# Neighbour averages with three blocks of targets to a product instead of four

## The chip, the cores and the metric

The kernel runs on one core of a Trainium2 chip. The metric is the device time of one execution in microseconds. Before the change it was 3845.87 us, the median of three runs (3844.31 to 3850.38).

## What is computed

The reference is a small graph network on 6250 nodes with 128 features. There are 206,250 directed edges: 100,000 drawn pairs, both ways, and a loop on every node, sorted by target. A first part with two message layers is followed by a second part, in which each of three layers takes the mean of a node's neighbours. The second part is the one that matters here:

```python
def _L1_gnn_ref(x, edge_index, Wl, bl, Wr):
    src = edge_index[0]
    dst = edge_index[1]
    n = x.shape[0]
    deg = jax.ops.segment_sum(jnp.ones(src.shape[0], dtype=x.dtype), dst, num_segments=n)
    inv_deg = (1.0 / jnp.maximum(deg, 1.0))[:, None]
    h = x
    for i in range(NUM_LAYERS):
        agg = jax.ops.segment_sum(h[src], dst, num_segments=n) * inv_deg
        h = agg @ Wl[i].T + bl[i] + h @ Wr[i].T
        if i < NUM_LAYERS - 1:
            h = jax.nn.relu(h)
    return h
...
x = x + _L0_gnn_ref(relu(layernorm(x)), edge_index, ...)
x = x + _L1_gnn_ref(relu(layernorm(x)), edge_index, ...)
```

## The kernel before

Nodes are cut into blocks of B = 128, which gives NB = 49 blocks. All of the work is in the function `fast`; a slow general way, `general`, is compiled too and not run on these data.

The first part sorts the edges of each target block and runs the two message layers (to 2913 us). In its second layer it also counts, for each pair of a source block and a target block, how many edges join each source to each target. These counts, 128 x 128 bytes for each pair of blocks, go to the array `cnt` in HBM, in the order target block, source, source block, target.

The second part, the averages (lines 731 to 787), turns every segment sum into dense products with these counts. For a group of n target blocks, `sums = sum over the 49 source blocks s of h[s]^T x cnt[s -> group]`, where the columns of a product are the n x 128 targets of the group. This document calls the work on one group a **pass**. The features `h` are kept as two parts (`h2`, the index k), which add up to the exact value, so that each source block takes two products: a pass has 2 x 49 = 98 products, all into one PSUM bank `p` of 512 columns, which is the reason for at most four blocks. `spans` lists the groups as (first block, number of blocks): eleven groups of four, then one of three and one of two, since a last group of one is avoided. The three layers run over the same list.

In the order of the code, a pass does the following:

- Every R = 8 source blocks it loads the counts of its n target blocks into a byte tile `c8` (L767). The load stands on SP's queue. There are three buffers (the pool `mats` has `bufs=3`), so seven loads per pass, the last one for a single source block.
- Every K = 4 source blocks it turns the bytes into 32-bit numbers, `cf` (L771). ScalarE and VectorE take turns at this cast through the whole stage (`turn`); a pass has 13 casts, so that the engine that begins alternates from pass to pass. `cf` too has three buffers, and the last cast of a pass, of a single source block, takes a whole one.
- After every third source block it calls `next(behind, None)`, which lets the work on the previous pass's nodes go one step on.
- It issues the two products of the source block (L779).

At the end of a pass what is left of the previous pass's `behind` is finished, and a new one begins for this pass: `averaged` copies the PSUM bank to `sums` on ScalarE (L737), then takes the n blocks one after the other. For each, TensorE multiplies by `Wl` (L742, two instructions), VectorE scales by the inverse degree and adds the rest, giving `u` (L744); in the first two layers `mean_rows` follows, with a rounding of `u` to `h2` on ScalarE (L264) and its remainder on VectorE (L265), a transpose on TensorE (L268), a copy of it on ScalarE (L270), and the product with `Wr` (L273, two instructions) whose result VectorE adds to the bias (L274). In the third layer there is instead a load of `x1d` (L750), an addition (L751) and the store of the output (L753), both DMAs on SP's queue. The document calls this the **side work** of a node block. In the trace it is interleaved with the products, six products from one step to the next, and the first L742 of a pass comes after four or ten of its products.

Each engine takes its instructions in order. What is behind a waiting instruction on the same queue waits too.

Of the kernel before, what the change touches and what calls it, by code (L numbers as in the profile page):

```python
# [45 lines left out]
@with_exitstack  # L46
def gnn_kernel(ctx: ExitStack, tc: tile.TileContext, x, src, dst, weights, columns, rows, out, edges):

    nc = tc.nc
    dram = ctx.enter_context(tc.tile_pool(name="dram", bufs=1, space=DRAM))
    const = ctx.enter_context(tc.tile_pool(name="const", bufs=1))
    ident = const.tile([D, D], F32, name="ident")
    make_identity(nc, ident)
    miss_i = const.tile([1, 1], I32, name="miss_i")
    fast(tc, dram, ident, miss_i, x, src, dst, weights, columns, rows, out, edges)  # L60
    tc.strict_bb_all_engine_barrier()
    missed = nc.values_load(miss_i[0:1, 0:1], min_val=0, max_val=1,
                            skip_runtime_bounds_check_because="a comparison's result")
    with tc.If(missed > 0):
        general(tc, dram, ident, x, src, dst, weights, columns, rows, out)


def fast(tc, dram, ident, miss_i, x, src, dst, weights, columns, rows, out, edges):
    nc = tc.nc
    N = x.shape[0]  # L70
    NB = N // B
# [9 lines left out]
    with ExitStack() as ctx:  # L81
# [672 lines left out]
                yield  # L754

        turn = 0
        spans = [(g, min(4, NB - g)) for g in range(0, NB, 4)]
        if spans[-1][1] == 1:
            spans[-2:] = [(NB - 5, 3), (NB - 2, 2)]
        for l in range(3):  # L760
            for g, n in spans:
                p = bank("pe")
# [253 lines left out]
```

## Time and profile before

| | |
|---|---|
| median of the runs | 3845.87 us |
| the profiled execution: its time | 3845.1 us |
| the profiled execution: its span, first to last instruction | 3843.3 us |
| busy: TensorE, VectorE, ScalarE | 98%, 76%, 66% of the span |
| mean granted clock of TensorE | 0.996 |
| the averages: from their first product to the last | 2912.99 us to 3831.2 us |
| DMA in the averages | 118 to 158 GB/s in the slices wholly of that stage |

The stage splits by layer and by pass as follows. Each figure is the time from the first product of a pass to the first of the next, by the starts in the trace (of the very last, to the end of its last product).

| | first pass | passes of four after it | pass of three | pass of two | whole layer |
|---|---|---|---|---|---|
| first layer | 24.75 us | 10, 25.14 to 25.22 us | 20.12 us | 16.25 us | 312.9 us |
| second layer | 25.69 us | 9, 25.13 to 25.22 us, and one of 25.46 | 19.66 us | 14.43 us | 311.8 us |
| third layer | 24.45 us | 10, 23.82 to 23.83 us | 18.14 us | 12.60 us | 293.5 us |

A pass of four in the first two layers holds 98 products and the side work of four node blocks (8 instructions of L742, 4 of L268, 8 of L273). The pass of three and the pass of two carry the nodes of the pass before them, so four and three. The second and the third layer begin with the two nodes of the last pass of the layer before. The idle time at the end of the first layer is 2.13 us, and at the end of the second 0.57 us; both lie in the figures of the passes of two.

How to read it: TensorE is the engine to follow. A row of the groups gives the line, engine and operation, the tiles and shapes, the number of instructions, then the busy time, the mean duration of one and the idle time of the engine ahead of them with what ended it. The chain of waits follows the work that ended last back through whatever released it. In the timeline, columns are the start in us, the duration in us, the engine, the line and the operation; what ended an idle time is in brackets.

### The profile page before, as it was taken

The page shows a single profiled execution, that of the slowest core. Times are in us where ns is not written, and L with a number is a line of the kernel's source. Part 1 is how long each engine was busy: PE and PEld are TensorE (multiplying, and loading weights), DVE is VectorE, ACT ScalarE, POOL GpSimd, SP SyncE. Part 2 cuts the span into 40 slices and gives each one's busy share as a digit, 9 for nine tenths or more (in the row PEclk, how much of TensorE's full clock was granted, in tenths as well). Part 3 has the DMA queues.
Part 4 walks back from the last instruction along what each step waited for, and adds up shares of the span by engine and source line. Part 5 has one row for each costly group of instructions (what it writes and reads, how often), then busy time and mean ns, then how long its engine had stood idle before and what let it go on. Part 6 is the DMA issues. An engine that isn't in the chain of part 4 may idle for free.

```text
span 3843.3 us, 117274 instructions
## 1 busy us (share of the span) xinstructions
PE 3785.3 (98%) x45975; PEld 3570.6 (93%) x45975; DVE 2901.7 (76%) x7367; ACT 2522.5 (66%) x4869; POOL 1.0 (0%) x8
## 2 busy tenths in 40 slices
PE   6999999999999999999999999999999999999998
PEld 4999999999999999999999999999998888888887
DVE  8999999999999997787777778787874444444443
ACT  7565666566655665777877788787875555555554
POOL 0000000000000000000000000000000000000000
PEclk9999999999999999999999999999999999999999
DMA  4555555555555555677777777777774444444554
GB/s 139 161 166 169 170 175 164 168 172 175 165 168 170 173 170 169 204 212 213 215 212 215 211 217 210 212 216 213 214 212 136 131 129 118 129 128 121 157 158 131
DMA packets 656081, 671.11 MB, mean 175 GB/s; under 512 B 113201, under 2 KB 504475, under 8 KB 655387
## 3 DMA queue, kind: packets, MB, share of 16 engines
q1 hardware_dynamic: 650124, 662.26, 57.8%
q8 instruction: 362, 5.93, 0.6%
q10 hardware_dynamic: 5390, 1.26, 0.2%
q14 instruction: 205, 1.67, 0.1%
HBM read 534.28 MB, written 128.99 MB: 173 GB/s over the span
## 4 chain that ended last, share of the span: by engine, by line
PE 96%; DVE 2%; DMA 1%; ACT 1%; issue 0%; SPq 0%; DVEq 0%; ACTq 0%
PE pe L779 22%; PE pe L563 21%; PE pe L565 21%; PE agg L583 21%; PE so L522 4%; PE so L418 2%; PE mm L273 1%; PE agg L742 1%; PE mm L600 1%; PE mm L601 1%; PE mm L252 1%; PE mm L268 0%; DMA a<-in_x 0%; PE mm L616 0%; PE mm L595 0%
## 5 line engine op out<-in xcount | busy, mean ns | idle before, releaser
L563 PE MATMUL pe<-a,ot 128*128 128x128 bf16 x14700 | 1626.2, 219 | 0.0
L565 PE MATMUL pe<-b,ot 128*128 128x128 bf16 x14700 | 1620.5, 219 | 0.0
L563 PEld LDWEIGHTS <-ot 128*128 128x128 bf16 x14700 | 1036.5, 98 | 33.2
L565 PEld LDWEIGHTS <-ot 128*128 128x128 bf16 x14700 | 1026.6, 98 | 0.0
L779 PE MATMUL pe<-cf,h 128*128 128x512 f32 (+2 forms) x3822 | 911.3, 391 | 2.7 <-ACT cf L771 2.0
L779 PEld LDWEIGHTS pe<-cf,h 128*128 128x128 f32 x3822 | 675.3, 189 | 131.8 <-ACT cf L771 2.6
L572 ACT ACTIVATE m<-pe 128x512 fp32r<-128x512 f32 (+1 forms) x882 | 507.6, 576 | 321.0 <-PE pe L565 277.1
L489 DVE TENSOR_SCALAR ot<-v_all,part 128x1024 bf16<-128x1024 bf16 (+1 forms) x1274 | 599.4, 471 | 145.2 <-PE pe L565 127.6
L771 ACT CAST cf<-c 128x2048 fp32r<-128x2048 uint8 (+4 forms) x253 | 433.7, 1714 | 330.4 <-PE pe L779 273.8
L583 PE MATMUL agg<-m,hd_r 128*128 128x256 f32 (+1 forms) x3332 | 613.0, 303 | 0.5 <-DVE m L552 0.5
L552 DVE SCALAR_TENSOR_TENSOR m<-pe,m 128x512 fp32r<-128x512 f32 (+1 forms) x882 | 577.3, 655 | 18.8 <-ACT m L572 5.1
L771 DVE CAST cf<-c 128x2048 fp32r<-128x2048 uint8 (+4 forms) x254 | 285.7, 1125 | 351.8 <-PE pe L779 212.7
L583 PEld LDWEIGHTS agg<-m,hd_r 128*128 128x128 f32 x3332 | 452.0, 190 | 1.0 <-DVE m L552 0.9
L583 PE MATMUL agg<-m,hd 128*128 128x129 f32 x3136 | 434.5, 281 | 0.0
L514 ACT CAST hd_r<-hd_b 128x512 fp32r<-128x512 bf16 (+1 forms) x637 | 393.2, 618 | 2.0 <-DMA hd_b<-ohd 2.0
L583 PEld LDWEIGHTS agg<-m,hd 128*128 128x128 f32 x3136 | 380.9, 191 | 0.0
L524 ACT CAST ca<-so 128x512 uint8<-128x512 f32 (+1 forms) x637 | 358.9, 563 | 0.0
L514 ACT CAST hd<-hot 128x512 f32<-128x512 bf16 x392 | 242.7, 619 | 169.6 <-DVE hot L88 66.5
L575 ACT ACTIVATE m<-pe 128x512 f32<-128x512 f32 x392 | 234.0, 597 | 143.5 <-PE pe L565 141.7
L88 DVE TENSOR_TENSOR hot<-sv,iota 128x512 bf16<-128x512 f16 (+1 forms) x637 | 249.3, 404 | 29.3 <-ACT hd_r L514 22.2
L88 DVE TENSOR_TENSOR hs<-sources,iota 128x512 bf16<-128x512 f16 (+1 forms) x637 | 259.1, 407 | 2.8 <-PE so L522 1.5
L522 PE MATMUL so<-hd_b,hs 128*128 128x128 bf16 x2450 | 244.3, 219 | 2.1 <-DMA hd_b<-ohd 1.5
(162 smaller groups left out, 3136.6 us busy)
## 6 DMA issues: line engine op xcount, KB each, us to landing
v_all<-svd SPq DMA_DIRECT2D x1176, 256.0 KB, 3.9
c<-cnt SPq DMA_DIRECT2D x198, 512.0 KB, 3.7
ohd<-hot SPq DMA_DIRECT2D x588, 128.0 KB, 3.6
hd_b<-ohd SPq DMA_DIRECT2D x588, 128.0 KB, 3.7
cnt<-ca SPq DMA_DIRECT2D x540, 64.0 KB, 3.7
v_all<-svd SPq DMA_DIRECT2D x98, 128.0 KB, 3.2
c<-cnt SPq DMA_DIRECT2D x18, 384.0 KB, 3.2
c<-cnt SPq DMA_DIRECT2D x18, 256.0 KB, 2.8
```

Of the source, the lines that this page charges most:

```text
L88: nc.vector.tensor_tensor(to, v.rearrange("p (r e) -> p r e", e=2).unsqueeze(2).to_broadcast([B, n, B, 2]), iota_2.unsqueeze(1).to_broadca ...
L489: nc.vector.tensor_scalar(t[:, :n].rearrange("p j k s -> p (j k) s"), v[:, :2 * n], part, None, op0=OP.is_equal)
L514: nc.scalar.copy(hd[:, :n].rearrange("p (r e) v -> p r e v", e=2), hot[:, :n // 2].rearrange("p r v e -> p r e v"))
L522: nc.tensor.matmul(pa[:, j * B:(j + 1) * B], source[:, j // 2, :, j % 2], target[:, j // 2, :, j % 2], start=True, stop=True)
L524: nc.scalar.copy(ca[:, :n], pa[:, :n * B].rearrange("p (j d) -> p j d", d=B))
L552: nc.vector.scalar_tensor_tensor(m[:, :n, :D], pe, 0.0, m[:, :n, D:2 * D].bitcast(F32), op0=OP.max, op1=OP.subtract)
L563: nc.tensor.matmul(pe[:, o], t[:, j, 0, :], a3[l][:, block, k, :], start=(k == 0), stop=False)
L565: nc.tensor.matmul(pe[:, o], t[:, j, 1, :], b3[:, k, :], start=False, stop=(k == 2))
L572: nc.scalar.activation(m[:, :n, D:2 * D], pe, AF.Relu)
L583: nc.tensor.matmul(to, hd[:, j, :], m[:, j, :to.shape[1]], start=(c == 0), stop=(c == NB))
L771: (nc.scalar.copy if turn % 2 else nc.vector.tensor_copy)(cf[:, :k, :n].rearrange("p s w d -> p w s d"), c8[:, :n, s % R:s % R + k])
L779: nc.tensor.matmul(p[:, :n * B], h2[l % 2][:, s, k, :], cf[:, s % K, :n].rearrange("p w d -> p (w d)"), start=(s == 0 and k == 0), stop=(s ...
```

## The change

The list of groups is built with three blocks to a group instead of four. For 49 blocks that gives groups that begin at 0, 3, ... 48, of which the last would hold one block; the last two are replaced by (45, 2) and (47, 2). So there are 15 passes of three and two of two in each layer, 17 instead of 13. Nothing else in the code is changed: tiles and buffers keep their sizes, a product has 384 columns instead of 512, a load brings 384 KB instead of 512 KB, and a cast turns 1536 numbers per partition instead of 2048.

```diff
         turn = 0
-        spans = [(g, min(4, NB - g)) for g in range(0, NB, 4)]
+        spans = [(g, min(3, NB - g)) for g in range(0, NB, 3)]
         if spans[-1][1] == 1:
-            spans[-2:] = [(NB - 5, 3), (NB - 2, 2)]
+            spans[-2:] = [(NB - 4, 2), (NB - 2, 2)]
         for l in range(3):
             for g, n in spans:
                 p = bank("pe")
```

Per layer this makes 1666 products instead of 1274, 221 casts instead of 169, 119 loads of counts instead of 91, and 17 copies of sums instead of 13. The number of node blocks, and with it the side work, is 49 in either case.

## The prediction

> **What bounds the kernel now.** I read the page's chain of waits first, then the groups with shapes apart from 2900 us to the end, then the timeline of a few stretches.
>
> ```profile
> PE 96%; DVE 2%; DMA 1%; ACT 1%; issue 0%; SPq 0%; DVEq 0%; ACTq 0%
> ```
>
> TensorE sets the end. The chain gives L779, the products that the change reshapes, 22% of the span; they run from 2912.99 us on, and nothing before that is touched.
>
> ```profile
> L779 PE MATMUL pe<-cf,h 128*128 128x512 f32 x3234 | 815.2, 404 | 2.7 <-ACT cf L771 2.0 <-DVE cf L771 0.4 <-PE mm L616 0.3
> L771 ACT CAST cf<-c 128x2048 fp32r<-128x2048 uint8 x198 | 376.9, 1904 | 258.7 <-PE pe L779 229.8 <-issue 24.2 <-DVE u L744 2.3
> L771 DVE CAST cf<-c 128x2048 fp32r<-128x2048 uint8 x198 | 242.8, 1226 | 275.6 <-PE pe L779 158.7 <-ACT cf L771 86.5 <-issue 23.7
> L779 PE MATMUL pe<-cf,h 128*128 128x384 f32 x294 | 57.3, 344 | 0.0
> L779 PE MATMUL pe<-cf,h 128*128 128x256 f32 x294 | 39.7, 287 | 0.0
> L771 ACT CAST cf<-c 128x1536 fp32r<-128x1536 uint8 x18 | 26.5, 1475 | 20.1 <-PE pe L779 16.7 <-issue 3.4
> L771 DVE CAST cf<-c 128x1536 fp32r<-128x1536 uint8 x18 | 22.0, 1224 | 19.3 <-PE pe L779 16.5 <-issue 2.6
> L771 ACT CAST cf<-c 128x1024 fp32r<-128x1024 uint8 x18 | 18.9, 1048 | 16.5 <-PE pe L779 14.2 <-issue 2.3
> L737 ACT COPY sums<-pe 128x512 f32<-128x512 f32 x33 | 19.2, 583 | 7.9 <-PE pe L779 7.9
> L737 ACT COPY sums<-pe 128x384 f32<-128x384 f32 x3 | 1.4, 473 | 0.6 <-PE pe L779 0.6
> ```
>
> Two readings. Products hardly wait for casts (2.7 us in 3234) while casts wait for products, so casts have room. And each layer already has one pass of three blocks and one of two: the trace holds the new shapes, three passes of each. A matmul's mean (404 ns) overlaps its neighbours, so I price products by their spacing, from unbroken stretches of the chain:
>
> ```profile
> 3639.80 18.74 PE pe L779 x80
> ...
> 3805.91 12.65 PE pe L779 x73
> ...
> 3821.90 8.10 PE pe L779 x69
> ```
>
> That is 234.25 ns with 512 columns, 173.3 with 384, 117.4 with 256: per block of 128, 58.6, 57.8 and 58.7 ns.
>
> **The products.** A layer has now 11 passes of four, one of three, one of two, 98 products each: 98 x (11 x 234.25 + 173.3 + 117.4) = 281.0 us. Afterwards 15 of three and two of two: 98 x (15 x 173.3 + 2 x 117.4) = 277.8. That is 3.25 less per layer, 9.7 less in three, although 392 products per layer are added.
>
> [...]
>
> **Side work.** Behind each pass TensorE does the previous pass's nodes (L742, L268, L273). In the third layer two pairs of L742 start at 3661.63 and 3663.25 with six products between: 1.62 - 6 x 0.234 = 0.22 us per node. In the first two, steady passes of four last 25.13 to 25.22 us between their first products; less 98 x 0.234 = 22.96 that is 0.56 per node. Nodes stay 49 a layer, so this moves and costs nothing more. Even these passes hold no waiting.
>
> **Waits.** What a pass takes beyond products and side work, from the starts of first products:
> - passes of three: 20.12 - 16.98 - 4 x 0.555 = 0.91; 19.66 gives 0.45; third layer 18.14 - 16.98 - 0.88 = 0.27.
> - passes of two, without the idle end: 0.93, 0.67, and in the third layer about 0.42 with the last product's tail.
> - first passes: 1.44 (products 427 ns apart at the start), 1.62 and 0.38; one pass of four 0.28; idle ends of layers 2.13 and 0.57.
> Together 10.2 us now; the same ledger closes on the stage's length within 0.1.
>
> Where the 0.91 lies shows the mechanism:
>
> ```profile
> 3201.73 1.23 DVE L771 CAST cf<-c 128x1536 fp32r<-128x1536 uint8 x1 [0.41 <-PE pe L779]
> 3201.88 0.38 PE L742 MATMUL agg<-wt,sums 128*128 128x128 f32 x2
> ...
> 3202.87 0.34 DVE L744 SCALAR_TENSOR_TENSOR u<-agg,inv,hT 128x128 f32<-128x128 f32 x1
> ...
> 3203.26 0.33 PE L268 MATMUL mm<-ident,u 128*128 128x128 f32 x1
> ```
>
> L268 needs u, u is queued on VectorE behind a cast, and the six products between now last 1.04 us instead of 1.41; the next spacing was 295 instead of 173 ns, and at the third node 470. VectorE's cast of 1536 costs what 2048 costs (1224, 1226 ns): its share per pass rises while cover shrinks. Behind L268 all products queue in order. At a pass's start the first L742 waits for the sums copy (316 and 213 ns instead of 173 and 109), which shrinks with the copy, 0.58 to 0.47.
>
> A new pass of three carries three nodes, not four. The first three nodes of the two samples waited 0.61 and 0.41; less 0.1 for the shorter copy, between 0.3 and 0.5. Bounds: 0.1 (the start alone) and 0.9 (the worst sample at every pass). I take 0.45, nearer the samples' mean than either end. Third layer 0.2 (0.05 to 0.27). After: first passes 1.44 + 0.95 + 0.4; 28 x 0.45 = 12.6; 14 x 0.2 = 2.8; passes of two 0.8 + 0.55 in each of the first two layers, 0.67 in the third, 0.1 for the new handover from two to two.
>
> **Ends of layers.**
>
> ```profile
> 3223.93 1.90 ACT L771 CAST cf<-c 128x2048 fp32r<-128x2048 uint8 x1 [1.94 <-PE pe L779]
> ...
> 3225.88 1.48 PE L779 MATMUL pe<-cf,h 128*128 128x512 f32 x4 [1.96 <-ACT cf L771]
> ```
>
> ```profile
> c<-cnt SPq DMA_DIRECT2D x198, 512.0 KB, 3.7
> c<-cnt SPq DMA_DIRECT2D x18, 384.0 KB, 3.2
> c<-cnt SPq DMA_DIRECT2D x18, 256.0 KB, 2.8
> ```
>
> The named releaser is long done: the load was issued at 3220.09, when its buffer came free, and the cast began 3.83 later. With 384 KB the load is 0.5 and ScalarE's cast 0.43 shorter: idle 2.13 becomes about 1.2, and 0.57 (VectorE's cast first) about 0.06. After the 2.13 the layer's first products ran 427 ns apart; after 0.57 they did not. Whether 1.2 does is not in the trace: bounds 0 and 1.6 us, and I take half, which is the 0.95 above.
>
> [...]
>
> **Costed at nothing.** Loads rise from 91 to 119 per layer, 28 x 0.36 us on SP's queue, which is idle most of the stage; bytes stay. The tightest load is a pass's second: its buffer comes free with the cast of blocks 44 to 47 of the pass before, and from the release of that cast to its own cast 26 products pass, 4.5 us, less the 1.5 of the cast: 3.0, against 3.2 to land. The 0.2 is covered, since that cast is due 16 products (2.77) after the pass begins and needs 0.35 + 1.48 of them; in the third layer, where loads stand behind L750 and L753 on SP, a further 0.7 would be, and the rest paid in full. Four more copies on ScalarE per layer (0.47 each) lie under products; uncovered, 12 x 0.47 = 5.6.
>
> **Sum.** Waits after: 1.44 + 0.95 + 0.4 + 12.6 + 2.8 + 2.7 + 0.67 + 0.1 + 1.2 + 0.06 = 22.9, 12.7 more than 10.2. With -9.7 the stage is 3.0 longer: the profiled run of 3845.1 (span 3843.3) becomes 3848.1; that run lies 0.8 below the median 3845.87, which becomes **3848.8**.
>
> **Rivals.**
> - A, cheaper products without new waits. For: passes of four show none, so the order on the queues can be free of them. Against: all three passes of three show some. With 0.1 and 0.05 per pass: 3848.8 - 28 x 0.35 - 14 x 0.15 = 3836.9.
> - B, slower: u behind VectorE's cast at every pass. For: 0.91 in one sample, and a cast that does not shrink. With 0.9 per pass, 0.27 in the third layer: 3848.8 + 28 x 0.45 + 1 = 3862.4. It decides from about 0.6 per pass on.
> - C, slower: casts late at the start of a pass. The last block's lone cast takes a whole buffer, so the next pass's casts have 10 products' time, 1.73 us, against 1.475 on ScalarE; with 1.17 against 1.05, passes of two lost some 0.14 to 0.19, so the handover costs about 0.3 and three blocks just fit. Were it 0.5: 45 x 0.25 = 11 us, 3860.
> - D, the price of 173.3 does not hold and 384 columns cost what a line through 256 and 512 gives, 175.8: 4410 x 2.5 ns = 11, 3860. Against: 73 products in a row at 173.3.
> The change does what it says: 15 x 3 + 2 + 2 = 49 blocks.
>
> **How the numbers follow.** Forecast 0.55, A 0.12, B 0.22, C 0.05, D 0.06. The forecast's own range is 3842 to 3855 (0.25 to 0.65 per pass). The whole range leaves out most of A and the top of B: 3838 to 3862. No change means within 0.2%, 7.7 us, about what a measurement can tell: 3838.2 to 3853.6. Faster is A, 0.12; slower is B, C, D and 0.03 of the forecast, 0.36; the rest 0.52.
>
> **What would show it.** 4410 products with 384 columns at 173 ns in unbroken stretches (D if near 176); passes of three some 19.1 us long in the first two layers and 17.8 in the third (A at 18.7, B at 19.5); spacings before L268 and L273 longer than 173 (B), or before the fifth or ninth product of a pass (C); idle ends of 1.2 and 0.1 us. I would be wrong if casts or loads, not side work, filled the passes' extra time, or if work before 2913 us moved.

## The result, and the profile after

| | before | after |
|---|---|---|
| median of 20 runs of each on one chip | 3845.96 us (3841.03 to 3851.61) | 3852.48 us (3849.78 to 3857.04) |
| ratio after to before | | 1.0019 [1.0012, 1.0025] |
| profiled execution: time, span | 3845.1, 3843.3 us | 3851.8, 3850.0 us |
| start of the first product of the averages | 2912.99 us | 2912.72 us |
| **stage**: from there to the end of the last product | 918.2 us | 926.0 us |
| **tail**: from there to the end of the span | 12.1 us | 11.3 us |

The change makes the kernel 6.5 us slower: clear of zero, and by the medians just inside the 0.2% that the prediction called no change (the interval reaches 0.25%). The stage is 7.8 us longer, the tail 0.8 shorter, the start 0.27 earlier; that is the 6.7 us between the spans. TensorE still sets the end; VectorE's share of the chain of waits went from 2% to 3%:

```profile
PE 95%; DVE 3%; DMA 1%; ACT 1%; issue 0%; SPq 0%; DVEq 0%; ACTq 0%
```

The groups of the averages of the kernel after, shapes apart (instructions, then busy time and mean ns of one, then idle time before them):

```profile
L779 PE MATMUL pe<-cf,h 128*128 128x384 f32 x4410 | 835.1, 344 | 2.2 <-DVE cf L771 1.3 <-ACT cf L771 0.8
...
L771 ACT CAST cf<-c 128x1536 fp32r<-128x1536 uint8 x270 | 398.5, 1476 | 305.0 <-PE pe L779 227.3 <-issue 72.6 <-DMA c<-cnt 3.8
L771 DVE CAST cf<-c 128x1536 fp32r<-128x1536 uint8 x270 | 330.5, 1224 | 260.2 <-PE pe L779 227.4 <-DMA c<-cnt 19.1 <-issue 7.6
L779 PE MATMUL pe<-cf,h 128*128 128x256 f32 x588 | 78.0, 286 | 0.7 <-DVE cf L771 0.7
```

A product with 384 columns takes the 344 ns that it took before, and 79 of them in a row in the chain of waits last 13.71 us, so 173.5 ns each: the price that was forecast.

```profile
3637.87 13.71 PE pe L779 x79
```

ScalarE's cast shrank with the block, from 1904 to 1476 ns. VectorE's did not, 1226 to 1224, and VectorE now makes 270 of these where it made 198: it is busy longer for the same counts. The loads now end 19.1 us of the idle time ahead of VectorE's casts.

By passes, as in the table of before:

| | first pass | passes of three after it | passes of two | whole layer |
|---|---|---|---|---|
| first layer | 19.79 us | 13, 19.08 to 19.15 (by turns 19.15 and 19.12), one of 19.85 | 13.78, 14.53 us | 316.6 us |
| second layer | 18.38 us | 13, 19.13 to 19.28, one of 19.53 | 14.27, 13.54 us | 314.8 us |
| third layer | 18.60 us | 13, 17.79 to 17.85, one of 18.40 | 13.53, 12.32 us | 294.5 us |

Products by their spacing are 3 x 277.8 = 833.3 us. With side work at the prediction's 0.555 and 0.22 us per node, some 65 us, the waits of the stage are 27.5 us: 10.2 before, 22.9 forecast.

**Where a pass waits.** Three places, each read in the timeline of the kernel after (start, duration, engine, line, operation; in brackets the idle time before it and what ended it). First, the start of a pass:

```profile
3007.51 1.48 ACT L771 CAST cf<-c 128x1536 fp32r<-128x1536 uint8 x1 [1.30 <-PE pe L779]
...
3009.05 0.65 PEld L779 LDWEIGHTS pe<-cf,h 128*128 128x128 f32 x4 [0.20 <-ACT cf L771]
3009.21 0.48 ACT L737 COPY sums<-pe 128x384 f32<-128x384 f32 x1 [0.21 <-PE pe L779]
```

ScalarE's cast could begin only when a buffer of cf came free, and its end is what the next weight load and product waited for: one spacing of 280 ns instead of 173, 0.107 us in every pass of three. Second, in every other pass:

```profile
3017.22 0.38 PE L742 MATMUL agg<-wt,sums 128*128 128x128 f32 x2
...
3017.42 1.22 DVE L771 CAST cf<-c 128x1536 fp32r<-128x1536 uint8 x1 [0.76 <-PE pe L779]
3018.56 0.34 DVE L744 SCALAR_TENSOR_TENSOR u<-agg,inv,hT 128x128 f32<-128x128 f32 x1
...
3018.96 0.33 PE L268 MATMUL mm<-ident,u 128*128 128x128 f32 x1
```

L742 gives agg, but u (L744) is queued on VectorE behind a cast that began first, and L268, on which every later product waits, starts only with u: 470 ns instead of 173 in front of it, 0.35 us in all. Third, in the passes between, uT (L270) is queued on ScalarE behind a cast of 1.48 us in the same way, and L273 waits:

```profile
3033.55 1.48 ACT L771 CAST cf<-c 128x1536 fp32r<-128x1536 uint8 x1 [1.90 <-issue]
...
3034.00 0.27 PE L268 MATMUL mm<-ident,u 128*128 128x128 f32 x1
...
3035.14 0.26 ACT L270 ACTIVATE uT<-mm 128x128 f32<-128x128 f32 x1
...
3035.45 0.49 PE L273 MATMUL mm<-wt,uT 128*128 128x128 f32 x2
```

Its spacings are 280 to 310 and 213 ns in place of 173 and 109, about 0.22 us, and 0.3 together with smaller delays at L742 and at the end of the pass. Beyond its products and three nodes at the prediction's 0.555 us, a pass of three in the first two layers lasts 0.48 us longer, and in the third, where there is no L268 or L273 and a node counts 0.22 us, 0.18.

Not all of that is waiting. By the starts in the two traces, where nothing waits, the steps of a node (L742, L268, L273) stretch the products by 0.57 us in a pass of three and by 0.54 in a pass of four. Counted so, side work is some 3 us longer after the change than before (67.0 and 63.8 us), and the waits of a steady pass of three are 0.43 to 0.46 us. No run tells why the steps became dearer.

**Where single passes wait.** The 19.85 us pass of the first layer:

```profile
3164.04 1.48 ACT L771 CAST cf<-c 128x1536 fp32r<-128x1536 uint8 x1 [1.28 <-DMA c<-cnt]
...
3165.63 0.26 ACT L270 ACTIVATE uT<-mm 128x128 f32<-128x128 f32 x1
...
3165.94 0.49 PE L273 MATMUL mm<-wt,uT 128*128 128x128 f32 x2 [0.43 <-ACT uT L270]
```

This pass's second load was issued at 3159.32 and its cast could start only 4.7 us later, where a pass's other second loads take 3.3 to 3.7 as a rule. The cast then stood in front of uT, and L273 waited 0.70 us beyond the usual. In the third layer a wait for a store stands in front:

```profile
3711.55 0.35 DVE L744 SCALAR_TENSOR_TENSOR u<-agg,inv,hT 128x128 f32<-128x128 f32 x1 [2.36 <-DMA out<-u]
...
3712.14 2.47 DVE L771 CAST cf<-c 128x1536 fp32r<-128x1536 uint8 x2
...
3713.41 0.66 PEld L779 LDWEIGHTS pe<-cf,h 128*128 128x128 f32 x4 [0.45 <-DVE cf L771]
```

u has two buffers; the store (L753) of the node two before had not finished, L744 held VectorE 2.36 us for it, and two casts went late behind it. This costs 0.58 us here and some 1.1 in the first pass of two of that layer, where one spacing of products is 998 ns. The store is not the whole of it: three_c8, below, changes only the room for loads. There L744 still waits 2.15 us for the store, and the pass of 18.40 us lasts 18.00.

### The profile page after: what moved, and what is told of

It reads as the page before. It is cut to its first block, busy times and chain, and to the rows that moved or that the text cites. A ratio compares the mean times of both kernels' runs of the same rounds, so it can differ in the third digit from the quotient of the medians.

```text
span 3850.0 us, 120136 instructions
## 1 busy us (share of the span) xinstructions
PE 3789.9 (98%) x47151; PEld 3711.1 (96%) x47151; DVE 2981.3 (77%) x7445; ACT 2536.9 (66%) x4959; POOL 1.0 (0%) x8
## 4 chain that ended last, share of the span: by engine, by line
PE 95%; DVE 3%; DMA 1%; ACT 1%; issue 0%; SPq 0%; DVEq 0%; ACTq 0%
PE pe L563 21%; PE pe L779 21%; PE pe L565 21%; PE agg L583 21%; PE so L522 4%; PE so L418 2%; PE mm L273 1%; PE agg L742 1%; DVE cf L771 1%; PE mm L600 1%; PE mm L601 1%; PE mm L252 1%; PE mm L268 1%; PE mm L595 0%; PE mm L616 0%
## 5 line engine op out<-in xcount | busy, mean ns | idle before, releaser
L779 PE MATMUL pe<-cf,h 128*128 128x384 f32 (+1 forms) x4998 | 912.6, 337 | 3.0 <-DVE cf L771 2.0
L779 PEld LDWEIGHTS pe<-cf,h 128*128 128x128 f32 x4998 | 825.1, 189 | 13.9 <-ACT cf L771 5.9
L771 ACT CAST cf<-c 128x1536 fp32r<-128x1536 uint8 (+3 forms) x331 | 448.8, 1356 | 367.2 <-PE pe L779 284.0
L771 DVE CAST cf<-c 128x1536 fp32r<-128x1536 uint8 (+2 forms) x332 | 369.0, 1112 | 330.3 <-PE pe L779 293.9
```

The costliest lines, as they stand in the source:

```text
L771: (nc.scalar.copy if turn % 2 else nc.vector.tensor_copy)(cf[:, :k, :n].rearrange("p s w d -> p w s d"), c8[:, :n, s % R:s % R + k])
L779: nc.tensor.matmul(p[:, :n * B], h2[l % 2][:, s, k, :], cf[:, s % K, :n].rearrange("p w d -> p (w d)"), start=(s == 0 and k == 0), stop=(s ...
```

## The experiments

The start of the stage lay between 2912.7 and 2919.5 us in the profiled executions of these kernels, although the code before it is the same. A difference of a few us is therefore read from the stage and its passes, and the medians are set beside it. Each stage is that of one profiled execution: its steady passes agree within some hundredths of a us, but a single late pass need not come back in the next. By the medians only three_best and three_best_v are clear of the kernel after, as their intervals and its (1.0012 to 1.0025) do not overlap.

| kernel | median | ratio to before | stage | tail |
|---|---|---|---|---|
| three_cf4 | 3855.20 us | 1.0024 [1.0014, 1.0033] | 924.5 us | 13.4 us |
| four_cf4 | 3843.56 | 0.9989 [0.9980, 0.9998] | 915.8 | 13.6 |
| three_noside | 3785.49 | 0.9842 [0.9827, 0.9857] | 858.6 | |
| four_noside | 3791.02 | 0.9858 [0.9843, 0.9873] | 861.3 | |
| three_c8 | 3853.34 | 1.0016 [1.0007, 1.0025] | 922.9 | 11.2 |
| three_split | 3851.57 | 1.0007 [0.9998, 1.0016] | 921.4 | 11.2 |
| three_order | 3847.59, one run | | 920.4 | 11.3 |
| four_c8cf4 | 3845.18 | 0.9988 [0.9979, 0.9997] | 914.2 | 13.9 |
| three_four | 3853.42 | 1.0016 [1.0007, 1.0025] | 920.9 | 15.3 |
| three_best | 3846.95 | 0.9999 [0.9990, 1.0008] | 915.4 | 12.9 |
| three_best_v | 3844.43 | 0.9993 [0.9984, 1.0003] | 915.7 | 12.8 |
| four_best | 3839.61 | 0.9983 [0.9974, 0.9992] | 911.4 | 12.3 |

Names with "three" start from the kernel after, with "four" from the kernel before.

**A fourth buffer for cf**, alone, in both kernels.

```diff
-                        cf = mats.tile([B, K, 4, B], F32R, name="cf")
+                        cf = mats.tile([B, K, 4, B], F32R, name="cf", bufs=4)
```

> A fourth buffer for cf, passes of three as in the change. Theory (cast lead): at each pass start one product spacing of about 280 instead of 173 ns is a wait for ScalarE's cast of 1.48 us, which had only ten products (1.73 us) for itself and its handover; with a fourth buffer it has eight products more, so these spacings fall to 173 and 42 passes lose 0.107 us each: 4.5 us less, a median near 3848. The waits of L268 and L273 behind VectorE's cast stay (about 0.35 us a pass in the first two layers). Rival (side work alone makes the passes longer): no change, 3852, and the 280 ns stay.

> The kernel before with a fourth buffer for cf, as a control. Both theories: a cast has ten products of 234 ns, 2.34 us, against 1.90 on ScalarE, and no spacing is stretched at a pass start, so nothing changes: 3846, passes of four 25.1 to 25.2 us. A gain of over 2 us would say that the buffer helps whatever the number of blocks.

The spacings of 280 ns at the start of a pass vanished, and the passes did not get shorter: 19.11 and 19.19 us by turns, 19.15 on average, 17.83 and 17.85 in the third layer. The timeline of three_cf4 says why:

```profile
3011.37 1.48 ACT L771 CAST cf<-c 128x1536 fp32r<-128x1536 uint8 x1 [1.30 <-PE pe L779]
...
3012.76 0.47 ACT L737 COPY sums<-pe 128x384 f32<-128x384 f32 x1
3013.28 0.30 PEld L742 LDWEIGHTS agg<-wt,sums 128*128 128x128 f32 x2 [0.22 <-ACT sums L737]
```

The copy of the sums stands behind that cast on ScalarE, and L742 now waits for it (242 and 214 ns in place of 173 and 109). The buffer was not the limit; ScalarE's queue is, one cast and one copy long. In the kernel of four the steady passes stay at 25.13 to 25.24 us, and the gain lies around the end of the first layer (its pass of two from 16.25 to 14.44, the second layer's first from 25.69 to 24.50): 2.4 us of stage.

**Without the side work of the first two layers**, in both.

```diff
-            for j in range(n):
+            for j in range(n if l == 2 else 0):
...
-                        nc.tensor.matmul(p[:, :n * B], h2[l % 2][:, s, k, :],
+                        nc.tensor.matmul(p[:, :n * B], h2[0][:, s, k, :],
```

> Leaves out the side work of the first two layers (L742 to L274; every layer takes the first layer's features), with passes of three. Theory (products are cheaper, side work makes the loss): passes of three last 98 x 173.3 ns + 0.11 = 17.1 us in the first two layers, and the first two layers together are about 3 us shorter than in the kernel with passes of four and the same work left out. Rival (each product has a fixed part, so that more of them cost more): over 17.3 us a pass, and the first two layers longer than with passes of four.

> Leaves out the side work of the first two layers (L742 to L274; every layer takes the first layer's features), with passes of four. Theory: passes of four last 98 x 234.25 ns = 22.96 us in the first two layers; the first two layers together are about 3 us longer than with passes of three. Rival (fixed part in each product): the first two layers are shorter than with passes of three.

Passes of four became 22.95 to 22.96 us and passes of three 17.09 to 17.10, with the 0.107 at the start as all that is left beyond 98 x 0.1733 = 16.98. The chains of waits (start, duration, engine, line, number of products), first of three_noside:

```profile
2999.88 31.08 PE pe L779 x178
...
3032.48 4.56 DMA c<-cnt
...
3037.12 1.48 ACT cf L771
```

and of four_noside:

```profile
2999.93 110.09 PE pe L779 x470
```

That is 174.6 and 234.2 ns, 58.2 and 58.6 per block: without side work three at a time is the cheaper shape. The two layers are 1.8 us shorter with three (566.98 against 568.82), and would be 4.2 shorter but for four passes of 17.4 to 18.1 us that hold a late load like the one in the chain above. The forecast for the products of two layers, 6.5 us, less 28 times the 0.107, is 3.5. So the products are cheaper as forecast, and the larger part of what a pass loses, 0.37 of 0.48 us, comes with the side work.

**A fourth buffer for c8** in the kernel after; then c8 and cf together in the kernel before.

```diff
-                        c8 = mats.tile([B, 4, R, B], U8, name="c8")
+                        c8 = mats.tile([B, 4, R, B], U8, name="c8", bufs=4)
```

> A fourth buffer for c8, passes of three as in the change; the order on TensorE, VectorE and ScalarE is the same. Theory: single passes that last 0.3 to 0.7 us more than their neighbours, and the idle ends of the first two layers (1.0 and 0.57 us), come from loads that have only 3.0 us between buffer and cast; with one set more they have 2.8 us longer, so these go, some 2.5 to 3.5 us, and no pass of three in the first two layers exceeds 19.3 us. The steady 19.13 us (0.11 at ScalarE's first cast, 0.35 at the side work) stays. Rival (loads also cause the steady part): steady passes fall below 19.0.

> The kernel before with four buffers each for c8 and cf. Theory: its steady passes hold no waits, so they keep 25.13 to 25.22 us; the idle ends of the first two layers (2.13 and 0.57 us) and the half-speed products after the first (1.4 us) go, some 3 to 4 us: 3842 to 3843. Rival (load times do not set the ends): 3846.

Nothing in the order of work on TensorE, VectorE or ScalarE differs from the kernel after. The steady passes are unchanged, and but for the first pass of all (19.74 us) no pass of three in the first two layers is over 19.20 us. The place of the late load, in three_c8:

```profile
3170.59 0.28 ACT L270 ACTIVATE uT<-mm 128x128 f32<-128x128 f32 x1 [0.15 <-PE mm L268]
...
3171.44 0.38 PE L273 MATMUL mm<-wt,uT 128*128 128x128 f32 x2
```

uT follows L268 at once, and L273 waits for nothing. The passes at the ends of the layers went from 14.53 to 13.98 and from 13.54 to 13.18 us, two of the third layer from 18.40 to 18.00 and 13.53 to 13.20; the stage is 3.1 shorter. The median does not show it (1.0016 against 1.0019); in the profiled execution the stage began at 2918.85, 6 us later. In the kernel of four, both buffers together take 4.0 us from the stage.

**VectorE's cast cut in two**, so that u waits for half a cast.

```diff
-                        (nc.scalar.copy if turn % 2 else nc.vector.tensor_copy)(
-                            cf[:, :k, :n].rearrange("p s w d -> p w s d"), c8[:, :n, s % R:s % R + k])
+                        if turn % 2 or k == 1:
+                            (nc.scalar.copy if turn % 2 else nc.vector.tensor_copy)(
+                                cf[:, :k, :n].rearrange("p s w d -> p w s d"), c8[:, :n, s % R:s % R + k])
+                        else:
+                            for c in range(0, k, 2):
+                                nc.vector.tensor_copy(cf[:, c:c + 2, :n].rearrange("p s w d -> p w s d"),
+                                                      c8[:, :n, s % R + c:s % R + c + 2])
```

> VectorE's casts of four source blocks are cut into two of two. Theory (u is queued behind VectorE's cast): u waits for 0.6 to 0.7 instead of 1.22 us at most, so the 470 ns spacing before the third L268 of every second pass falls to under 250 and these passes from 19.15 to 18.8 to 18.9 us; the others, whose wait is before L273 behind ScalarE's work, stay at 19.1. Some 3 to 5 us less in all. Rival (L268 waits for something else): 470 stays and the passes keep 19.15 us.

The passes in which u waited went from 19.15 to 18.80 to 18.83 us, the others stayed at 19.15 to 19.17, and the stage is 4.6 us shorter, although VectorE's work grew (two casts of 685 ns for one of 1224). This shows the place where half of the passes lose: u behind the cast.

**The same cast with its dimensions in another order**: the four source blocks outermost, not the three targets.

```diff
-                            cf[:, :k, :n].rearrange("p s w d -> p w s d"), c8[:, :n, s % R:s % R + k])
+                            cf[:, :k, :n], c8[:, :n, s % R:s % R + k].rearrange("p w s d -> p s w d"))
```

> The casts run through source block, target block, target instead of target block, source block, target; the order on TensorE is the same. If VectorE's 1224 ns for 1536 numbers (as much as for 2048) is a matter of the order in which it goes through them, they fall towards 0.6 ns each, 920 ns, and the wait before L268 shrinks by 0.3 us in every second pass; if it is not, 1224 and 19.15 us stay.

The group of VectorE's casts and the timeline, of three_order:

```profile
L771 DVE CAST cf<-c 128x1536 fp32r<-128x1536 uint8 x270 | 258.9, 959 | 287.4 <-PE pe L779 263.6 <-issue 10.1 <-DMA c<-cnt 8.9
```

```profile
3017.86 0.38 PE L742 MATMUL agg<-wt,sums 128*128 128x128 f32 x2
...
3018.05 0.96 DVE L771 CAST cf<-c 128x1536 fp32r<-128x1536 uint8 x1 [0.76 <-PE pe L779]
3018.93 0.34 DVE L744 SCALAR_TENSOR_TENSOR u<-agg,inv,hT 128x128 f32<-128x128 f32 x1
...
3019.33 0.33 PE L268 MATMUL mm<-ident,u 128*128 128x128 f32 x1
```

From L742 to L268 it is now 1.47 us, against 1.74 in the kernel after: the cast is 0.265 shorter, and the spacing in front of L268 fell from 470 to 214 ns. Passes are 18.90 and 19.12 us by turns, the stage 5.6 us shorter. The passes that gained 0.25 make 3.5 of that; most of the rest is that the late passes of 19.85 and 18.40 us did not come back (18.98 and 17.81), and that is not shown to be the order's doing. ScalarE's cast keeps its 1477 ns, and so do the passes in which uT waits behind it.

**One pass of four at the end of each layer** in place of two of two.

```diff
-            spans[-2:] = [(NB - 4, 2), (NB - 2, 2)]
+            spans[-2:] = [(NB - 4, 4)]
```

> Only the end of each layer differs from the change: 15 passes of three and one of four instead of two of two; the products take the same 277.8 us a layer. Theory: what passes of two wait (2.5, 2.0 and 1.7 us in the three layers beyond products and side work, idle ends among it) goes, and one pass of four with some 0.3 takes its place: 5 us less in the stage, 921 us from the first product to the last instead of 926. Passes of three keep 19.13 us. Rival (the last four blocks cost nothing extra): 926.

The stage was 920.9 us, as expected, and the time did not follow. After the last product four node blocks are left instead of two. The end of three_four in its timeline:

```profile
3834.75 0.58 ACT L737 COPY sums<-pe 128x512 f32<-128x512 f32 x1 [3.60 <-PE pe L779]
...
3838.42 0.82 DVE L744 SCALAR_TENSOR_TENSOR u<-agg,inv,hT 128x128 f32<-128x128 f32 x2 [1.50 <-DMA out<-u]
...
3839.89 0.82 SPq L753 DMA_DIRECT2D out<-u  x2
```

The third and fourth node wait 1.50 us for the store buffers of the first two, and the tail is 15.3 us instead of 11.3. With a stage that began 1.1 us later, that takes back all of the 5.1 us that the stage had lost.

**Together.** three_best is three_four with the other order of the cast and four buffers each for c8, u and xw; three_best_v has a fourth buffer for cf as well, and VectorE copies the sums:

```diff
-            nc.scalar.copy(s[:, :n * B], p[:, :n * B])
+            nc.vector.tensor_copy(s[:, :n * B], p[:, :n * B])
```

four_best is the kernel before with ten passes of four and three of three, the other order, and four buffers each for c8, cf, u and xw:

```diff
-            spans[-2:] = [(NB - 5, 3), (NB - 2, 2)]
+            spans[-3:] = [(NB - 9, 3), (NB - 6, 3), (NB - 3, 3)]
```

> Passes of three with one of four at the end, casts in the order that takes VectorE 959 ns, four buffers for c8, u and xw. Theory: the causes add up: 926 less 5 (passes of two), 4 to 5 (order of the casts) and 2 (late loads, stores that hold VectorE): a stage of 914 to 916 us, as long as passes of four with more buffers (914.2). Rival (one cause moves into the next): over 918.

> As the kernel with passes of three, one of four, quick casts and four buffers for c8, u and xw, with a fourth buffer for cf too and the sums copied by VectorE. Theory: the 0.11 to 0.14 us at each pass start are ScalarE's cast and copy in one queue; with the copy on VectorE and the fourth buffer both go: 42 x 0.11 = 4.6 us less than that kernel, a stage of 910 us, below every version with passes of four. Rival (VectorE then delays u and the casts): no gain.

> Ten passes of four and three of three, four buffers for c8, cf, u and xw, casts in the other order. Theory: no idle ends, no passes of two; products 98 x (10 x 234.25 + 3 x 173.3) = 280.5 us a layer, side work 27 us and 10.8 us in the third, waits some 0.4 in each pass of three: a stage of 912 to 914 us. Rival: the same 918 us as before.

three_best gave the stage that was expected, 915.4 us, with passes of 18.90 and 19.13, and the time of the kernel before within its interval: repaired, three at a time only draws level. In three_best_v the second expectation held: passes of 19.20 and 19.00 us, no gain in the first two layers, since the copy (554 ns on VectorE, 476 on ScalarE) only moved the queue to the other engine. four_best beats both kernels, 6.4 us under the runs of before beside it (0.9983 [0.9974, 0.9992]): steady passes stay at 25.13 to 25.23 us, and the gain lies at the ends of the layers. It can't be told from four_cf4 and four_c8cf4 by the intervals, only by its stage.

## Why the prediction came out as it did

It said 3848.8 us, slower by 2.9 and not to be told from no change; measured are 3852.48 and 6.5. The mechanism was right in the main and a part of the sizes was not. That the time is still inside the band of no change is in part luck: 3.7 us above the forecast, it stands just below the upper bound of 3853.6.

- **The products**: -9.7 us at 173.3 ns. Right; 173.5 in unbroken stretches, and the pair without side work shows a gain with little of its cost.
- **Side work moves only.** Nearly: by the starts of products a node's steps add 0.57 us where they added 0.54, some 3 us in all, which the ledger at 0.555 us counts among the waits.
- **Waits per pass of three**, 0.45 and 0.2 us. Right: 0.48 and 0.18. Where they come from was half told. u behind VectorE's cast was named, and three_split and three_order show it, but only in every other pass. uT behind ScalarE's cast in the passes between costs some 0.3 us and wasn't named; no run removed it alone, so it is read from the timeline. Rival B's price of 0.9 at every pass is refuted. Rival C was judged to just fit, and its wait is there in every pass, 0.107 us; three_cf4 shows that freeing the buffer doesn't give it back, since the sums copy queues behind the same cast.
- **"Costed at nothing"** is the step that was furthest off. The second load of a pass was given 3.0 us against 3.2 to land, "the 0.2 is covered", and a further 0.7 in the third layer too. That is a median against a margin. Single loads took up to 4.7 us, and cost 0.70 and some 0.6 in two layers; three_c8, which changes nothing but the room for loads, leaves no pass of three over 19.20 us in these layers behind the first of all. Waiting for stores wasn't in that step at all: in the third layer a node's L744 waits for an earlier store and holds VectorE's casts, 0.58 and about 1.1 us together with the loads' part in it. That is some 3 us of the 4.6 by which the waits were under-estimated.
- **First passes**: 1.44, 0.95 and 0.4 forecast; 2.26, 0.29 and 0.51 measured. In the first, L268 waits for z (L238), which is queued behind a VectorE cast: 607 ns instead of 173. The second ran its products some 173 ns apart behind the idle end, at a granted clock of 1.00, which saves 0.66 against the 0.95 taken (half of its bound of 1.6 would have been 0.8). This is luck as far as the runs tell: the last section shows that such an end can go either way.
- **Ends of layers**: 1.2 and 0.06 us forecast, 1.0 and 0.57 measured. The second didn't close: the load took 3.20 us to its cast where it had taken 3.71, as forecast, but it was issued 3.79 us before the layer's last product began, where it had been 4.30. three_c8 shortens both passes (by 0.55 and 0.36 us).
- The rest, some 0.8 us, is 28 times the 0.03 between 0.45 and 0.48.

## What to carry to other kernels

When a block shrinks, list for each engine what shrinks with it and what does not: a short step of a dependent chain that shares an in-order queue with long casts has its cover cut in proportion, and pays when the cast keeps its length (here six products cover 1.04 us in place of 1.41, the cast stays at 1224 ns, and the spacing before L268 goes from 173 to 470 ns). A ring of buffers is sized by its slowest transfers and not by their median, and a margin below nothing is a cost, however well the next work seems to cover it (here one load of 384 KB had its cast only 4.7 us after its issue, where 3.2 us to land had been counted on). And the last group of a loop sets the tail: what a different grouping saves among the passes can come back behind the last one (in three_four the tail is 15.3 us, not 11.3).

## What the runs showed of the hardware

VectorE's casts of counts to 32 bits follow 161 ns + 0.52 ns for each number per partition at 256, 512, 1024 and 2048 numbers (294, 427, 693 and 1226 ns). With three blocks outermost they don't: 1536 numbers take 1224 ns, which is 0.69 ns each beyond the 161, and 768 take 685, 0.68 each; 384, where the target is one unbroken run and the source three, take 553, 1.02 each. With four outermost 1536 take 959, on the line again. So 4/3 of the price per number with three outermost and twice the price in the last case. ScalarE's cast shows nothing of it (1476 and 1477 ns in the two orders).

The cast that did not shrink is thus no constant of the engine, since another order takes 959 ns, and the prediction's row of 1224 held only for its order. Why three blocks outermost cost more than four, no run shows.

At the end of the first layer TensorE's products stood still for 1.0 us in the kernel after and then ran on some 173 ns apart, at a granted clock of 1.00; in the kernel before they were 427 ns apart in place of 234 after 2.13 us. The length of the idle time does not decide this alone. In four_noside the products stood still as long (2.26 us between two starts, 2.24 in the kernel before) and then ran 231 to 238 ns apart. What differs is the clock granted to TensorE. Rows of 2 us behind both ends, first of before, then of four_noside (busy time of PE, PEld, DVE, ACT and POOL with instructions, then the granted clock as a share, the DMA's share and GB/s):

```profile
3228.00:3230.00 2.00, 2.00 (x6) 1.54 (x5) 0.59 (x2) 0.48 (x2) 0.00 (x0) 0.50 0.46 161
```

```profile
3200.00:3202.00 2.00, 2.00 (x10) 1.60 (x9) 0.31 (x1) 1.78 (x1) 0.00 (x0) 1.00 0.75 214
```

In before the clock stood at 0.5 from 3226.61 us on, for 3.41 us. In both traces it is 0.5 for another 3.41 us at the start of the stage (from 2912.58 us in before, 2913.16 in after), and from there to the end of the stage the kernel after shows 1.00 throughout. What set it off behind this end is not shown, nor whether other executions of before have it. By the second layer's first pass (25.69 us, against 24.50 in four_cf4 and 24.26 in four_c8cf4) it is worth 1.2 to 1.4 us of the stage.
